# Spectra stage of a fused four-layer kernel: images 0 and 2 placed in the input's tile, the last sample's normalisation moved to ScalarE, a new order of the score products

## The chip, the cores and the metric

The kernel runs on one core of one Trainium2 chip. The metric is the device time of one launch in microseconds (us), the median of several runs. Engines are named as in the profile: PE is TensorE, PEld its weight loads, DVE is VectorE, ACT is ScalarE, POOL is GpSimd, SP is the queue that issues most DMAs.

## The reference, cut to what matters

The input x is (4, 56, 56, 128). Four layers follow, each `x = x + layer(group_norm(x))`: window attention, an edge layer (a message per pair of 56 positions), a spectral attention layer, and a convolution with sums over time and agents. The change lies at the border of the second and third layers and in the first part of the third:

```python
x = x + _L1_conv_ref(_gn(x), ...)          # edge layer
x = x + _L2_conv_ref(_gn(x), ...)          # spectral attention
# inside _L2_conv_ref, _forward:
xa_n = _inorm(xa, norm_g[0], norm_b[0])    # per image (b, t): mean and variance over 56 x 128
k = _fno_layer(xa_n, wK, ..., (H // 2, W // 2))   # rfft2, 16 x 16 modes, weights per head, irfft2
q = _fno_layer(xa_n, wQ, ..., (H // 2, W // 2))
v = _fno_layer(xa_n, wV, ..., (H, W))
scores = einsum('bhtd,bhsd->bhts', qs, ks) / sqrt(d)
attn_w = softmax(scores)                   # 32 heads, 56 x 56 per head and sample
out = einsum('bhts,bhsd->bhtd', attn_w, vs)
# ... then a projection, two more spectral layers with norms, and the residual
```

B is 4 samples; P is 128 channels, on the partitions; HH is 56. One sample is one tile of 128 x 3136 f32, 1568 KB. The kernel never builds k, q and v: it works on the spectra of the images, with the weights of q and k multiplied beforehand.

## The kernel before, in words

**First two layers.** `build` runs `first_layers` once per sample: `fast_layer` (window attention, reads the input tile `xw`) and then `edge_layer`, which works in place on tile `x1`. The result goes to DRAM as `x2d`. Sample b - 1 is normalised for the third layer inside sample b's `fast_layer` by the generator `normed_images`, and written twice, as `xad[b]` and, transposed, as `xat[b]`. All this stands inside a runtime branch (`tc.If`). For the last sample, b = 3, this normalisation is left for the next stage. `xw` lies in the pool `io`, which is released after the branch. In the last edge layer nothing reads `xw` any more.

**Loading.** After the branch, `images(b)` loads `xad[b]` into a tile of pool `x2` in two halves on SP (rows 0 to 28, 29 to 55) and clears one more row on POOL (L2894). The pool has two buffers, so images 0 and 1 are loaded at once, and image 2 goes to the buffer of image 0 when that is free. Image 3 is `x1`.

**Spectra.** `spectra` (L1660 on) has an order written out by hand for PE, ACT and DVE; POOL and SP are ordered by the framework. Three generators are interleaved:

- `norm` is `normed_images` for sample 3: 28 steps of row statistics (`bn_stats`, L1525), then a chain of small operations with four tiny matmuls, then `apply_norm` (L193) on four strips of 128 x 784, the write of `xat[3]` and the factor `st.norm[:, 3, 1]`. `go_on(n)` advances it n steps.
- `first[b]` is `first_transform` of image b, four stages of 56 matmuls (L1616), each with one DVE product (L1618) and one ACT copy (L1620) into tile `s_z`.
- `sample_spectra` of sample b has 13 stages: three with the products for S and iS (L1632, copied out by ACT at L1635), two for R (L1644), eight for xh (L1654, copied out by DVE and ACT in turn, L232 and L230). After its stages 2, 5, 7 and 9 one stage of `first[b + 1]` is issued.

`fill(n)` issues n matmuls on constants (L1682), whose result nobody reads. In the same time POOL prepares weights (`score_weights`, `value_weights`, L1711 to L1769), from DRAM tensors that SP loads (L158), and SP writes their last product as `dd` (L1732).

**Scores.** `attention_weights` walks over a list `seq` of 72 products: for each pair of samples bp (0, 1) and each column c of 16, an item n = 0, whose operand `q_u` DVE makes (L1825), and an item n = 1, whose operand POOL makes (L1823); four more items per pair have theirs from DVE (L1821). Each is 16 matmuls (L1838) into `q_acc`. Operands are made four items ahead. After the last item of pair 0, `collect` (L1857) adds the sums into `sc`, and the generator `softmax` of pair 0 is appended to the list `between`. From the fourth item on each item is followed by one step of `between`: first the steps of `skips` (L1849, L1852), then, in pair 1, softmax steps: max, subtraction (L1864) and exponential (L1865) of two samples, sum and division (L1870 to L1872) of two, and four sets of transposes on PE (L1880) with a copy on ACT (L1882).

After that comes `attend` (L1984 and others) and then `outputs`, which the diff does not touch.

Of the kernel before, what the change touches and what calls it, by code (L numbers as in the profile page):

```python
# [19 lines left out]
P = 128  # L20
# [1492 lines left out]
def normed_images(k, w, st, b, wk, bank, xp, xad, xat):  # L1513

    nc = k.nc

    def tiny(name):
        return wk.tile([P, HH], F32, name="s_" + name, bufs=1)  # L1520

    x = xp[:, :HH, :]
    rows = wk.tile([P, HH, 6], F32, name="s_rows", bufs=1)
    for t in range(HH):
        nc.vector.bn_stats(rows[:, t, :], x[:, t, :])  # L1525
        if t % 2 == 1:
            yield
    mv = wk.tile([P, 2], F32, name="s_mv", bufs=1)
    nc.vector.bn_aggr(mv, rows.rearrange("p a b -> p (a b)"))
    yield  # L1530
    yield
    ps = bank()
    nc.tensor.matmul(ps[:, 0:1], k.g4, mv[:, 0:1], start=True, stop=True)
    yield
    mr = wk.tile([P, 2], F32, name="s_mr", bufs=1)
    t1 = wk.tile([P, 1], F32, name="s_t1", bufs=1)
    nc.vector.tensor_copy(mr[:, 0:1], ps[:, 0:1])
    nc.vector.tensor_sub(t1, mv[:, 0:1], mr[:, 0:1])
    nc.vector.scalar_tensor_tensor(t1, t1, t1, mv[:, 1:2], ALU.mult, ALU.add)
    yield  # L1540
    yield
    ps = bank()
    nc.tensor.matmul(ps[:, 1:2], k.g4, t1, start=True, stop=True)
    yield
    var = wk.tile([P, 1], F32, name="s_var", bufs=1)
    nc.vector.tensor_copy(var, ps[:, 1:2])

    half = [rows[:, :, i] for i in range(6)]
    mean, sq, d = tiny("mean"), tiny("sq"), tiny("d")
    nc.vector.tensor_sub(d, half[1], half[4])  # L1550
    yield
    nc.vector.tensor_mul(d, d, d)
    nc.vector.tensor_add(sq, half[2], half[5])
    yield
    nc.vector.scalar_tensor_tensor(sq, d, HH / 4, sq, ALU.mult, ALU.add)
    nc.vector.tensor_add(mean, half[1], half[4])
    yield "root"
    nc.scalar.activation(t1, var, AF.Sqrt, bias=k.eps)
    yield
    yield  # L1560
    nc.vector.reciprocal(mr[:, 1:2], t1)
    nc.vector.tensor_scalar(mean, mean, 0.5, mr[:, 0:1], ALU.mult, ALU.subtract)
    nc.vector.tensor_scalar_mul(mean, mean, mr[:, 1:2])
    yield
    nc.vector.tensor_scalar(sq, sq, mr[:, 1:2], mr[:, 1:2], ALU.mult, ALU.mult)
    ps = bank()
    nc.tensor.matmul(ps[:, 2:2 + HH], k.ones_c, mean, start=True, stop=True)
    yield
    nc.vector.tensor_copy(st.norm[:, b, 0, :], ps[:, 2:2 + HH])
    nc.vector.tensor_sub(d, mean, st.norm[:, b, 0, :])  # L1570
    yield
    nc.vector.tensor_mul(d, d, d)
    nc.vector.scalar_tensor_tensor(sq, d, float(HH), sq, ALU.mult, ALU.add)
    yield
    ps = bank()
    nc.tensor.matmul(ps[:, 62:62 + HH], k.ones_px, sq, start=True, stop=True)
    yield
    nc.vector.tensor_copy(d, ps[:, 62:62 + HH])
    yield

    def normed():
        for t in range(0, HH, 14):
            apply_norm(k, x[:, t:t + 14, :], x[:, t:t + 14, :], mr)
            if t < 42:
                yield
        nc.sync.dma_start(xat[b].rearrange("t w h -> w t h"), x)
        if b < B - 1:
            nc.sync.dma_start(xad[b], x)

    if b == B - 1:  # L1590
        yield from normed()
    yield "root"
    nc.scalar.activation(d, d, AF.Sqrt, bias=k.eps)
    yield
    yield
    nc.vector.reciprocal(d, d)
    nc.vector.tensor_scalar_mul(st.norm[:, b, 1, :], d, w.ng[:, 0:1])
    yield
    if b < B - 1:
        yield from normed()  # L1600


def first_transform(k, st, b, pools, x, to):

    nc = k.nc
    wk, psum = pools

    z = to[b] = wk.tile([P, 33, 2 * HH], F32, name="s_z")  # L1610
    xf = x.rearrange("p t h -> p (t h)")
    for t0 in range(0, HH, 14):
        ps = psum.tile([P, 512], F32, tag="row", name="s_pr")
        for t in range(14):
            for ri in range(2):
                nc.tensor.matmul(ps[64 * ri:64 * ri + 64, t * 33:(t + 1) * 33],  # L1616
                                 xf[:, (t0 + t) * HH:(t0 + t) * HH + 64], k.fw[:, ri, :], start=True, stop=True)
        nc.vector.tensor_mul(z[:, :, t0:t0 + 14], ps[:, :462].rearrange("p (t f) -> p f t", t=14),  # L1618
                             bc(st.norm[:, b, 1, t0:t0 + 14], 1, 33))
        nc.scalar.copy(z[:, :, HH + t0:HH + t0 + 14], z[:, :, t0:t0 + 14])  # L1620
        yield
# [38 lines left out]
def spectra(k, w, st, xat, images):  # L1660

    nc, tc = k.nc, k.tc
    for t in (st.S, st.iS, st.R):
        nc.gpsimd.memset(t[:, :, :, HH:], 0.0)
    nc.gpsimd.memset(st.x1[:, HH, :], 0.0)
    with ExitStack() as es:
        wk = es.enter_context(tc.tile_pool(name="s_wk", bufs=2))
        psum = es.enter_context(tc.tile_pool(name="s_ps", bufs=3, space=PSUM))  # L1670
        tiny = es.enter_context(tc.tile_pool(name="s_pt", bufs=1, space=PSUM))
        es.enter_context(tc.manual_schedule(engines={mybir.EngineType.PE, mybir.EngineType.Activation,
                                                     mybir.EngineType.DVE}))
        norm = normed_images(k, w, st, B - 1, wk, lambda: tiny.tile([P, 512], F32, name="s_pt"), st.x1, None, xat)
        zs = {}
        first = [first_transform(k, st, b, (wk, psum), st.x1 if b == B - 1 else images(b), zs) for b in range(B)]
        idle = tiny.tile([P, 512], F32, name="s_pt")

        def fill(n):

            for _ in range(n):
                nc.tensor.matmul(idle[:, :3 * P], k.ident, bc(k.ones, 1, 3), start=True, stop=True)  # L1682

        def go_on(n):
            for _ in range(n):
                next(norm, None)
        fill(3)
        go_on(28)
        next(first[0])
        next(first[0])  # L1690
        go_on(1)
        fill(4)
        next(first[0])
        go_on(1)
        next(first[0])
        go_on(2)
        for b in range(B):
            for n, _ in enumerate(sample_spectra(k, st, b, (wk, psum), zs.pop(b))):
                go_on(2)
                if b < B - 1 and n in (2, 5, 7, 9):  # L1700
                    next(first[b + 1])

# [69 lines left out]
def attention_weights(k, I, w, st):  # L1772
# [9 lines left out]
    with ExitStack() as es:  # L1782
# [20 lines left out]
        seq = []  # L1803
        for bp in range(2):
            for c in range(16):
                seq += [(bp, c, 0, None), (bp, c, 1, None)]
                if c in (8, 10, 12, 14):
                    seq.insert(len(seq) - 1, (bp, None, c // 2 % 2, c // 12))

        def make(bp, c, n, b2):  # L1810

# [77 lines left out]
        for n, item in enumerate(seq):  # L1889
# [4 lines left out]
            if item[1:3] == (15, 1):  # L1894
                for i in range(2):
                    collect(item[0], i)
                if item[0] == 0:
# [1 line left out]
                    make(1, 1, 1, None)  # L1899
                    between.append(softmax(0, lambda: psum.tile([P, 4, P], F32, tag="t", name="q_pt", bufs=1),  # L1900
                                           nc.vector.tensor_sub, nc.vector.tensor_mul))
            if n >= 3 and between and next(between[0], 0) == 0:
                between.pop(0)
        for steps in between:
            for _ in steps:
# [892 lines left out]
def build(k, packs, I, out):  # L2798
# [3 lines left out]
    with ExitStack() as es:  # L2802
# [7 lines left out]
        x1p = x1s.enter_context(tc.tile_pool(name="x1p", bufs=1, side="right"))  # L2810
        x1w = x1p.tile([P, HH + 1, HH], F32, name="x1")
        x1 = x1w[:, :HH, :]
        dd = dp.tile([3, 4, 2, 16, NB], F32, name="dd")

        l2p = es.enter_context(tc.tile_pool(name="l2", bufs=1))
# [1 line left out]
        st.x1 = x1w  # L2817
        st.norm = l2p.tile([P, B, 2, HH], F32, name="norm")
        with tc.tile_pool(name="w01", bufs=1) as wp, tc.tile_pool(name="io", bufs=1) as io:
            xw = io.tile([P, TOK], F32, name="xw")  # L2820
            with ExitStack() as pre:
                xs = pre.enter_context(tc.tile_pool(name="i_x", bufs=B - 1))
                x = [xw] + [xs.tile([P, TOK], F32, name="i_x") for _ in range(B - 1)]
# [25 lines left out]
                nc.vector.scalar_tensor_tensor(k.shift, k.mr[:, :, 0], -1.0, k.mr[:, :, 1], ALU.mult, ALU.mult)  # L2849
                small_scores = scores_are_small(k, bounds, wp, wk)  # L2850

            def first_layers(front, x, to, loaded=False):
                if not loaded:
                    nc.sync.dma_start(xw, x)
                xf = io.tile([P, TOK], F32, name="xf")
                st = io.tile([P, 9, 6], F32, name="x1_st")
                front(k, w0, xw, xf, x1, st)
                edge_layer(k, w1, x1, st)
                if to is not None:
                    nc.sync.dma_start(to, x1)  # L2860
# [12 lines left out]
            with small.Else():  # L2873
# [4 lines left out]
                with tc.tile_pool(name="n_x", bufs=2) as xs, tc.tile_pool(name="n_ps", bufs=2, space=PSUM) as psum:  # L2878
                    for b in range(B - 1):
                        xp = xs.tile([P, HH, HH], F32, name="n_x")  # L2880
                        nc.sync.dma_start(xp, x2d[b])
                        for _ in normed_images(k, w2, st, b, io, lambda: psum.tile([P, 512], F32, name="n_ps"), xp,
                                               xad, xat):
                            pass

        x2s = ExitStack()
        x2p = x2s.enter_context(tc.tile_pool(name="x2", bufs=2, side="right"))

        def images(b):
            if b not in loaded:  # L2890
                xp = loaded[b] = x2p.tile([P, HH + 1, HH], F32, name="s_x2")
                for o in (slice(0, 29), slice(29, HH)):
                    nc.sync.dma_start(xp[:, o, :], xad[b, :, o, :])
                nc.gpsimd.memset(xp[:, HH, :], 0.0)  # L2894
            return loaded[b]

        loaded = {}
        for b in range(2):
            images(b)
        nc.sync.dma_start(x2d[B - 1], x1)  # L2900
        l3p = es.enter_context(tc.tile_pool(name="l3", bufs=1))
        load_weights(k, l3p, I, "w3_", w2)
# [50 lines left out]
```

## Time and profile before

| what | value |
|---|---|
| median of the runs | 3492.82 us (3477.65 to 3494.12, 3 runs) |
| the profiled execution's own time | 3507.88 us |
| its span in the trace | 3505.9 us |
| mean granted PE clock | 0.983 |
| last edge layer ends | 2596.7 us |
| spectra stage | 2596.7 to 2694.6 us |
| scores, pair 0 and pair 1 | 2694.6 to 2764 us, 2764 to 2835 us |
| busy over the span | PE 95%, DVE 76%, ACT 61%, POOL 36% |

Times inside the kernel are microseconds from the start of the span of the profiled execution, which was 15 us longer than the median. The spectra and scores together are 239 us, some 7% of the span.

### The profile page before, as it was taken

The numbers are of one execution on the slowest core, as the hardware profiler recorded it, in microseconds if no ns is written. First come the engines' busy times: TensorE is split into PE (matmuls) and PEld (weight loads), VectorE is DVE, ScalarE is ACT, GpSimd is POOL, SyncE is SP. The second block draws the span as 40 slices with busy tenths as digits, with TensorE's granted clock in tenths as the row PEclk, the third lists the DMA queues.
The fourth block names the chain that finished last, engine by engine and source line by source line (L and its number), as shares of the span: only waits on it lengthen the run. The fifth ranks groups of instructions, "written<-read, shape, count | busy, mean of one in ns | idle before, by whom it ended". The sixth has DMA issues, their size and how long they took to land. (4 is left out here: it accounts for less than half of the span.)

```text
span 3505.9 us, 64398 instructions
## 1 busy us (share of the span) xinstructions
PE 3342.7 (95%) x27774; PEld 1447.5 (41%) x27774; DVE 2674.1 (76%) x2563; ACT 2130.6 (61%) x2251; POOL 1278.5 (36%) x784
## 2 busy tenths in 40 slices
PE   6999999999999999999999999999988999999998
PEld 4433333353333435333343543334346433336664
DVE  5588867868888696788859768885975778885766
ACT  4688876668888566788857578886642013215442
POOL 0000007700000590000029200001864778874776
PEclk8999999999999999999999999999998999999999
DMA  2134420023433000534400044332022047743201
GB/s 105 43 88 92 96 53 19 20 59 85 98 88 79 19 1 20 122 89 96 97 24 1 20 96 100 85 85 43 1 104 52 1 95 187 186 105 93 57 18 56
DMA packets 98014, 243.44 MB, mean 69 GB/s; under 512 B 64457, under 2 KB 69833, under 8 KB 92713
## 3 DMA queue, kind: packets, MB, share of 16 engines
q0 software_dynamic: 16128, 102.77, 14.7%
q1 hardware_dynamic: 74872, 123.61, 12.1%
q10 hardware_dynamic: 6720, 12.85, 1.3%
q8 instruction: 221, 3.62, 0.4%
q14 instruction: 73, 0.59, 0.1%
HBM read 79.43 MB, written 31.33 MB: 32 GB/s over the span
## 5 line engine op out<-in xcount | busy, mean ns | idle before, releaser
L830 ACT ACTIVATE f_ring<-f_pm 128x1792 f32<-128x1792 f32 (+1 forms) x764 | 1093.8, 1482 | 226.7 <-PE f_pm L827 179.7
L682 DVE TENSOR_TENSOR f_acc<-f_acc,f_ring 128x1792 f32<-128x1792 f32 x468 | 947.7, 2025 | 191.4 <-ACT f_ring L830 162.0
L827 PE MATMUL f_pm<-f_qT,f_kT 32*128 32x448 f32 x5376 | 723.0, 571 | 9.9 <-ACT f_p L716 4.1
L693 PE MATMUL f_pm<-f_ring,f_va 128*32 128x448 f32 (+1 forms) x6304 | 589.4, 490 | 0.0
L672 POOL DMA_DIRECT2D f_far<-f_ring x112 | 96.6, 862 | 1326.9 <-ACT f_ring L830 1071.8
L1230 POOL TENSOR_TENSOR e_tp<-e_a,e_c 128x1792 f32<-128x1792 f32 (+2 forms) x172 | 480.3, 2844 | 36.9 <-issue 36.9
L1228 DVE TENSOR_TENSOR e_td<-e_a,e_pc 128x1792 f32<-128x1792 f32 (+2 forms) x292 | 478.5, 1707 | 8.8 <-ACT e_c L1216 8.8
L827 PEld LDWEIGHTS f_pm<-f_qT,f_kT 32*128 32x128 f32 x5376 | 260.1, 183 | 412.0 <-ACT f_ring L830 300.8
L693 PEld LDWEIGHTS f_pm<-f_ring,f_va 128*32 128x32 f32 x6304 | 163.8, 109 | 410.1 <-issue 397.8
L1232 ACT ACTIVATE e_tp<-e_tp 128x1792 f32<-128x1792 f32 (+2 forms) x172 | 253.3, 1495 | 97.9 <-POOL e_tp L1230 97.9
L1979 DVE TENSOR_TENSOR u_ud<-u_px,u_d 112x1792 f32<-112x1792 f32 x144 | 263.5, 1864 | 39.8 <-PE u_po L1984 35.5
L1981 POOL TENSOR_TENSOR u_up<-xh,u_d 112x1792 f32<-112x1792 f32 (+1 forms) x72 | 241.0, 3375 | 55.2 <-PE u_po L1984 42.9
L1299 PE MATMUL e_acc<-e_td,t_edge 128*32 128x448 f32 x1952 | 231.6, 542 | 6.6 <-DVE e_td L1228 6.6
L1984 PE MATMUL u_po<-u_ud,AT 112*64 112x448 f32 x1056 | 213.8, 544 | 1.9 <-DVE u_ud L1979 1.9
L1299 PE MATMUL e_acc<-e_tp,t_edge 128*32 128x448 f32 x1184 | 147.9, 543 | 23.6 <-ACT e_tp L1232 23.6
L1984 PEld LDWEIGHTS u_po<-u_ud,AT 112*64 112x64 f32 x1056 | 74.5, 138 | 128.9 <-issue 112.9
L1299 PEld LDWEIGHTS e_acc<-e_td,t_edge 128*32 128x32 f32 x1952 | 61.7, 110 | 142.5 <-issue 93.8
L737 DVE RECIPROCAL f_den<-f_den 128x448 f32<-128x448 f32 x28 | 82.6, 2951 | 45.1 <-ACT f_den L734 45.1
L1823 POOL TENSOR_TENSOR q_u<-iS,q_g 128x1792 f32<-128x1792 f32 x32 | 102.8, 3235 | 28.4 <-PE q_acc L1838 28.4
L1838 PE MATMUL q_acc<-q_u,S 64*64 64x448 f32 x1024 | 106.5, 561 | 4.4 <-DVE q_u L1825 3.3
L813 POOL TENSOR_TENSOR x<-xf,xw 128x343 f32<-128x343 f32 x28 | 25.5, 910 | 226.5 <-DVE xf L802 226.5
L1984 PE MATMUL u_po<-u_up,AT 112*64 112x448 f32 x480 | 104.1, 547 | 2.4 <-POOL u_up L1981 2.4
(522 smaller groups left out, 4550.4 us busy)
## 6 DMA issues: line engine op xcount, KB each, us to landing
f_far<-f_ring POOLq DMA_DIRECT2D x112, 896.0 KB, 6.4
u_d<-dd SPq DMA_DIRECT2D x46, 784.0 KB
f_far<-f_ring SPq DMA_DIRECT2D x28, 896.0 KB
xw<-in_x SPq DMA_DIRECT2D x4, 1568.0 KB
x2d<-x SPq DMA_DIRECT2D x4, 1568.0 KB
xat<-x SPq DMA_DIRECT2D x4, 1568.0 KB
x_xs<-xat ACTq DMA_DIRECT2D x32, 196.0 KB
xm<-x_ev ACTq DMA_DIRECT2D x64, 98.0 KB
```

Source lines behind the costliest of these rows:

```text
L682: nc.vector.tensor_add(e.acc, e.acc, slots(j, c))
L693: nc.tensor.matmul(e.po[heads[h], part], va[o, c, heads[h]], p, start=(c == 0), stop=(c == 23 and part.stop == NB))
L827: nc.tensor.matmul(ss[:, i, :NB], kT[heads[h], c * P:(c + 1) * P], qT[heads[h], blk(j)], start=True, stop=True)
L830: nc.scalar.activation(ring[:, slot:slot + m, :], ss[:, :m, :NB], AF.Exp, scale=scale)
L1228: nc.vector.tensor_tensor(t, am, cm, ALU.max)
L1230: nc.gpsimd.tensor_sub(t, am, cm)
L1232: nc.scalar.activation(tf, tf, AF.Relu)
L1299: nc.tensor.matmul(acc[quarters[r0 + r], :NB], w.S[:, 0, :], t[:, r].rearrange("p l n -> p (l n)"), start=(g == 0), stop=(g == len(turns) ...
L1838: nc.tensor.matmul(acc[bp][i][halves[hb % 2], hb // 2, :NB], x[o], u[o, 8 * hb:8 * hb + 8, :].rearrange("p h t -> p (h t)"), start=first, ...
L1979: nc.vector.tensor_mul(u, bc(px[:, :, :NB], 2, m), dm)
L1981: nc.gpsimd.tensor_mul(u, bc(x, 2, m), dm)
L1984: nc.tensor.matmul(po[64 * b2:64 * b2 + 64, :NB], st.AT[:, 8 * i + h0 + q, 2 * bp + b2, :], u[:, b2, q, :], start=(left == 16), stop=(left ...
```

## The change

The input tile `xw` becomes a tile `xi` with one more row, in a pool of its own that lives until the end of the spectra. In the last sample's call of `first_layers`, between `fast_layer` and `edge_layer`, image 0 is loaded into it (one DMA on SP, one clear on POOL). After the branch only image 1 is loaded into `x2`, now one buffer. Image 2 goes into `xi` after the first transform of image 0, without a second clear.

The order of `spectra` begins with the four stages of `first[0]`, with four fills after the third, and no fills ahead of it. All steps of `norm` now come inside the samples: four per stage in stages 0 to 6 of sample 0, one per stage then, two per stage in stages 9 to 12 of samples 1 to 3. For sample 3 the four strips are normalised by ACT (`Identity` with a scale and a bias, the bias made by one more DVE operation on 128 x 1) in place of DVE.

In the scores, the item n = 1 of pair 0 comes one column later. In pair 1 a step of `between` is taken only at items 42, 46, 50 and so on to 70; one step is still taken at item 35.

```diff
@@ normed_images
+    if b == B - 1:
+        nc.vector.scalar_tensor_tensor(t1, mr[:, 0:1], -1.0, mr[:, 1:2], ALU.mult, ALU.mult)
...
-            apply_norm(k, x[:, t:t + 14, :], x[:, t:t + 14, :], mr)
+            if b == B - 1:
+                nc.scalar.activation(x[:, t:t + 14, :], x[:, t:t + 14, :], AF.Identity, bias=t1, scale=mr[:, 1:2])
+            else:
+                apply_norm(k, x[:, t:t + 14, :], x[:, t:t + 14, :], mr)
@@ spectra
-        fill(3)
-        go_on(28)
-        next(first[0])
-        next(first[0])
-        go_on(1)
-        fill(4)
-        next(first[0])
-        go_on(1)
-        next(first[0])
-        go_on(2)
+        for n in range(4):
+            next(first[0])
+            if n == 2:
+                fill(4)
+        images(2)
         for b in range(B):
             for n, _ in enumerate(sample_spectra(k, st, b, (wk, psum), zs.pop(b))):
-                go_on(2)
+                go_on(4 if b == 0 and n < 7 else 2 if b and n > 8 else 1)
@@ attention_weights
-                seq += [(bp, c, 0, None), (bp, c, 1, None)]
+                seq.append((bp, c, 0, None))
+                if bp or c:
+                    seq.append((bp, c - (not bp), 1, None))
                 if c in (8, 10, 12, 14):
                     seq.insert(len(seq) - 1, (bp, None, c // 2 % 2, c // 12))
+            if not bp:
+                seq.append((bp, c, 1, None))
...
-            if n >= 3 and between and next(between[0], 0) == 0:
+            if n >= 3 and between and (item[0] == 0 or n % 4 == 2 and n > 38) and next(between[0], 0) == 0:
@@ build
+        xwp = x1s.enter_context(tc.tile_pool(name="xw", bufs=1, side="right"))
+        xi = xwp.tile([P, HH + 1, HH], F32, name="xw")
+        xw = xi[:, :HH, :].rearrange("p t h -> p (t h)")
...
-            xw = io.tile([P, TOK], F32, name="xw")
...
+            def first_image():
+                nc.sync.dma_start(xi[:, :HH, :], xad[0])
+                nc.gpsimd.memset(xi[:, HH, :], 0.0)
...
                 front(k, w0, xw, xf, x1, st)
+                if to is None:
+                    first_image()
                 edge_layer(k, w1, x1, st)
...
-        x2p = x2s.enter_context(tc.tile_pool(name="x2", bufs=2, side="right"))
+        x2p = x2s.enter_context(tc.tile_pool(name="x2", bufs=1, side="right"))
...
-                xp = loaded[b] = x2p.tile([P, HH + 1, HH], F32, name="s_x2")
+                xp = loaded[b] = xi if b == 2 else x2p.tile([P, HH + 1, HH], F32, name="s_x2")
...
-                nc.gpsimd.memset(xp[:, HH, :], 0.0)
+                if b < 2:
+                    nc.gpsimd.memset(xp[:, HH, :], 0.0)
...
-        loaded = {}
-        for b in range(2):
-            images(b)
+        loaded = {0: xi}
+        images(1)
```

The other branch, which loads image 0 at its end, does not run with these inputs.

More of the change, by code (lines that the diff above doesn't have):

```diff
@@ L1610, in first_transform @@
     z = to[b] = wk.tile([P, 33, 2 * HH], F32, name="s_z")
-    xf = x.rearrange("p t h -> p (t h)")
+    xf = x().rearrange("p t h -> p (t h)")
     for t0 in range(0, HH, 14):
@@ L1675, in spectra @@
         zs = {}
-        first = [first_transform(k, st, b, (wk, psum), st.x1 if b == B - 1 else images(b), zs) for b in range(B)]
+        first = [first_transform(k, st, b, (wk, psum), lambda b=b: st.x1 if b == B - 1 else images(b), zs)
+                 for b in range(B)]
         idle = tiny.tile([P, 512], F32, name="s_pt")
@@ L2884, in build @@
                             pass
+                first_image()
         x2s = ExitStack()
-        x2p = x2s.enter_context(tc.tile_pool(name="x2", bufs=2, side="right"))
+        x2p = x2s.enter_context(tc.tile_pool(name="x2", bufs=1, side="right"))
         def images(b):
             if b not in loaded:
-                xp = loaded[b] = x2p.tile([P, HH + 1, HH], F32, name="s_x2")
+                xp = loaded[b] = xi if b == 2 else x2p.tile([P, HH + 1, HH], F32, name="s_x2")
                 for o in (slice(0, 29), slice(29, HH)):
                     nc.sync.dma_start(xp[:, o, :], xad[b, :, o, :])
-                nc.gpsimd.memset(xp[:, HH, :], 0.0)
+                if b < 2:
+                    nc.gpsimd.memset(xp[:, HH, :], 0.0)
             return loaded[b]
-        loaded = {}
-        for b in range(2):
-            images(b)
+        loaded = {0: xi}
+        images(1)
         nc.sync.dma_start(x2d[B - 1], x1)
```

## The prediction

> **What bounds the kernel now.** I read the page first (PE is busy 95% of the span, so a gain must come from stretches where PE waits or runs slowly), then the chain of work that ended last, to see where it leaves PE, then the busy times cut by windows. I cut at what the order of the code shows: `first[0]`, then samples 0, 1, 2, 3, then the two halves of the scores and the switch between them. Columns: stretch, its length, busy us (instructions) of PE, PEld, DVE, ACT, POOL, the granted clock, DMA.
>
> ```profile
> 2596.70:2617.00 20.30, 16.02 (x242) 11.77 (x241) 10.31 (x62) 1.74 (x3) 1.10 (x5) 0.83 0.86 293
> 2617.00:2649.30 32.30, 23.15 (x308) 20.17 (x307) 25.27 (x33) 7.29 (x17) 31.03 (x48) 0.80 0.24 96
> 2649.30:2668.20 18.90, 18.53 (x300) 15.40 (x300) 5.38 (x9) 8.70 (x19) 4.72 (x5) 0.89 0.67 125
> 2668.20:2684.80 16.60, 16.60 (x303) 14.69 (x302) 5.08 (x9) 7.70 (x17) 0.00 (x0) 1.00 0.02 4
> 2684.80:2694.60 9.80, 9.50 (x79) 7.86 (x78) 2.67 (x5) 6.04 (x14) 0.15 (x1) 1.00 0.02 5
> ...
> 2764.00:2788.00 24.00, 17.00 (x132) 8.20 (x128) 22.61 (x18) 4.94 (x6) 13.91 (x5) 0.86 0.00 1
> ```
>
> Sample 2 is the yardstick: 303 PE instructions in 16.6 us, no idle time, full clock. Sample 0 has 308 and takes 32.3; the 20.3 us ahead of it hold four stages that take 1.76 us each at full clock. So some 28 us of these 98 are waits and a low clock. The chain in the same window names them:
>
> ```profile
> 2601.51 2.53 issue
> 2604.04 4.74 PE s_pr L1616 x110
> 2608.78 4.71 PE s_pt L1682 x8
> 2613.49 3.41 PE s_pr L1616 x112
> ...
> 2627.10 3.16 PE s_pr L1616 x56
> ...
> 2631.05 13.19 DVE x L193
> ```
>
> L1616 costs 43 ns a matmul in the second line and 30 ns in the fourth: the first half ran at a low clock, as did the fills. Then 13.2 us of DVE in one `apply_norm`. The timeline shows that this is no work:
>
> ```profile
> 2622.46 1.26 DVE L1562 TENSOR_SCALAR s_mean<-s_mean,s_mr 128x56 f32<-128x56 f32 x1
> ...
> 2630.96 13.27 DVE L193 TENSOR_SCALAR x<-x,s_mr 128x784 f32<-128x784 f32 x1
> ...
> 2644.68 1.27 DVE L193 TENSOR_SCALAR x<-x,s_mr 128x784 f32<-128x784 f32 x2
> ```
>
> Two more strips take 1.27 us together; the first stood for 12.6 us while POOL worked without a gap on its weights. DVE is in order: `s_z` and `xh` queue behind the strip, and PE behind them. In the scores, the waits of PE:
>
> ```profile
> PE q_pt L1880 <- DVE y L1872: 5.9, 1, 5.9
> PE q_acc L1838 <- DVE q_u L1825: 3.3, 1, 3.3
> PE q_pg L1849 <- issue: 3.0, 1, 3.0
> ...
> PE q_acc L1838 <- DVE y L1857: 1.1, 1, 1.1
> ```
>
> At the switch of pairs a softmax step follows every product, and PE's transposes wait 5.9 us for DVE's division.
>
> [...]
>
> **The change, part by part** (gain positive, against this execution).
>
> *Image 0 loaded early.* One DMA of 1568 KB goes out on SP when `fast_layer` is done with `xw` (POOL's L815 at 2454.5), 140 us before it is needed; SP issues nothing else in the last edge layer. POOL's clear is 0.23 us in a POOL wait of 9.3 us ahead of L1230. Cost nothing; without that cover 0.23. After the branch SP issues two halves fewer (0.6 us each), so image 1, the write of `x2d` and the weights come sooner.
>
> *First transform.* Before: 20.3 us. After: 1.7 us from the branch to the first matmul, as now (2598.4); the 2.53 us "issue" gap, whose cause the trace does not show (between 0 and 2.5); four stages at 1.76 warm or 2.4 cold (4.74 x 56 / 110), 7.0 to 9.6; four fills, 2.6 warm (the first three took 2.17 with 6 records) to 4.8 cold. Together 11.3 to 18.6; I take 14.3. **Gain 6 (2 to 9).** The three fills and the 6.7 us of `bn_stats` that stood ahead of DVE's first `s_z` leave this place.
>
> *Sample 0.* Before: 32.3. After: the 16.6 of sample 2, plus two tiny matmuls (0.38 each), plus what PE waits for DVE: in stages 0 to 6 DVE has 6.7 us of statistics, two `s_z` (0.64) and a copy (0.61), 8.6 us, against 8.0 us of PE; `bn_aggr` adds 1.66. I take 1.5 us for these. Image 1's first half is needed 3.5 us into the sample, at about 2614; before, image 0's half landed 5 us after issue, so 2602 to 2606 is likely: nothing, at worst 2. No strip on DVE. Sum 19. **Gain 13 (10 to 15).**
>
> *Sample 1.* Before: 18.9, of which 2.3 is the clock. After: 16.6, two tiny matmuls (1.1), a wait for `s_mean` (1.4 before, L1562 to L1567) and one for `s_sq` (1.1 before). These fall at about 2637 to 2645, inside POOL's weights, which start when their loads land, near 2612 to 2617, and take 37 us as now. Then ACT's four strips, two after stage 9 or 10 and two after the next: the trace has no such ACT shape; between 0.58 (128x462, L1620) and 0.95 us (128x896, L1865) I take 0.85, 3.4 together. Behind them on ACT stand `s_z` and `xh` copies, then sample 2's S and iS copies; ACT had 7.7 us of work in 16.6, so it catches up; PE waits some 1.5 us (0 to 3). Sum 21.5. **Loss 2.5 (a loss of 14 to a gain of 1).** The lower end is the strip's own stall, met by L1562.
>
> *Samples 2 and 3.* Matmuls of `first[3]` need `x` and `st.norm` of sample 3: done at stage 0 of sample 2, used at stage 2. **Loss 0.5 (0 to 3).** The write of `xat[3]` is late by nothing: it is read in `attend`.
>
> *Image 2.* Its clear held POOL for 19.2 us before (L2894, until 2617.0); without it POOL's weights start on their data. Its load is issued near 2612 and lands by 2623; first used near 2635. Nothing.
>
> *Scores.* Pair 0's reorder moves nothing off a bound that I can see: PE's 3.0 us "issue" wait lies within `skips`, and POOL at 3.17 us a column keeps pace with PE at 3.1. **Nothing (a loss of 3 to a gain of 4).** Switch: the 24.0 us hold 112 to 116 matmuls of L1838 and 16 transposes. At the steady rate (128 matmuls in 12.31 us, 2788.01 on) that is 11.2, plus 2.6 for the transposes (0.65 each), 13.8; 1.9 us of waiting for `collect` stay. DVE then has, for four products (6.2 us), two operands at 2.02 and one step at 2.2 to 2.4, 6.4: just full, so I add 0.3. **Gain 8 (3 to 10).**
>
> Sum: 6 + 13 - 2.5 - 0.5 + 8 = 24 us, 3507.9 to 3484 for this execution. It was 15 us over the median of the runs, with nothing in it that the change touches as the reason; off the median: 3492.8 - 24 = **3469**. The forecast case by itself is 3459 to 3477.
>
> **Rivals.**
>
> *The lock moves.* L1562, L1563 or L1565 is passed over as the strip was: 12 us in sample 1, PE behind it at the matmul of `s_mean`. For it: they now meet the middle of POOL's work, where two chains of weights alternate. Against: before, L1562 met POOL too and lost 1 us. Gain 24 - 12 = 12: 3481.
>
> *The switch is bound by DVE anyway.* 6.4 us of DVE for 6.2 of PE leaves no room[...]. Gain in scores 2: 3475.
>
> *Slower: image 2 behind `dd`.* SP is in order and waited 31.5 us at L1732 for POOL's last weight; its order is the framework's. If image 2's load is put behind it, it leaves when POOL is done, 2649 to 2660, lands its half 5 us later, and PE stands in sample 1 from stage 2 on. With `dd` at 2660: resume at 2665, then 13.1 + 17.1 + 9.5 = 2704.7, 10.1 later than before, less 8 in the scores: 2 us slower, 3495. It decides from a `dd` later than 2658. Against: SP issued image 2 ahead of `dd` before, at 2616.97.
>
> *The change does not do what it says*: image 0 still waits for the branch's end. Then the first gain goes to 2 and the sum to 20: 3473.
>
> **Numbers.** Forecast 0.55; lock 0.16; switch 0.13; image 2 late 0.08; image 0 unchanged 0.04; something unseen and slower 0.04. From 3450 (the upper ends, 9 + 15 + 1 + 10 = 35 us, and half of the 15 us by which the lowest run lies under the median) to 3487 (the lock with a cold start) holds 8 in 10. About 0.5%, 17.5 us, is what a measurement of this kernel can tell from no change. Faster by more: 0.92 of the forecast, 0.35 of the lock, 0.7 of the switch and of the unchanged image, together 0.69, and 0.72 with some weight for the upper ends. Slower by more: the unseen and a quarter of the late image, 0.06. The rest, 0.22.
>
> **What would show each step.** First transform: `s_pr` from about 2599 without the fills, sample 0 from 2611. Sample 0: 19 us, clock near 1. Lock: an L1562 or L1563 of over 3 us. ACT's strips: four of 0.85 us. Scores: no wait of `q_pt` over 1 us, pair 1 about 61 us after its start. I am wrong if sample 0 stays over 25 us, if PE waits for image 2, or if the last half of the scores is no shorter.

## The result, and the profile after

The change makes the kernel faster: a median of **3473.45 us** (3467.87 to 3478.75) against 3493.33 us for the kernel before (12 runs each), a ratio of 0.994 with an interval of 0.9924 to 0.9956, so 15 to 27 us, and 19.9 by the medians. The profiled execution after took 3474.20 us, its span is 3472.3 us and its mean granted PE clock 0.988.

I cut both traces at the same events: the last product of the edge layer on DVE, the first S product of each sample on PE, the first copy of the scores on ACT, and the two sums of `collect`. All in us:

| stage | before | after | gain | forecast |
|---|---|---|---|---|
| edge layer's end to sample 0 | 20.87 | 24.77 | -3.9 | +6 |
| sample 0 | 31.73 | 16.95 | +14.8 | +13 |
| sample 1 | 19.01 | 17.04 | +2.0 | -2.5 |
| samples 2 and 3 | 26.54 | 27.36 | -0.8 | -0.5 |
| scores, pair 0 | 69.19 | 64.19 | +5.0 | 0 |
| scores, pair 1 | 69.23 | 61.57 | +7.7 | +8 |
| sum | 236.57 | 211.88 | +24.7 | +24 |

The spans differ by more, 33.6 us: the edge layer ended 1.1 us later and the rest of the program, which the diff does not touch, was 10.0 us shorter. That rest took between 660.3 and 672.6 us in the profiles of this document, without a pattern, so I don't count it.

The busy times of after, cut at these events. Columns: stretch, its length, busy us (instructions) of PE, PEld, DVE, ACT, POOL, the granted clock, DMA share, GB/s.

```profile
2597.85:2622.62 24.77, 15.62 (x235) 12.76 (x233) 2.62 (x7) 1.76 (x4) 12.73 (x29) 0.66 0.63 200
2622.62:2639.57 16.95, 16.95 (x305) 15.13 (x305) 13.91 (x68) 7.75 (x17) 16.85 (x23) 1.00 0.17 51
2639.57:2656.61 17.04, 17.04 (x308) 15.18 (x306) 8.96 (x24) 8.75 (x19) 4.55 (x5) 1.00 0.55 139
2656.61:2673.99 17.38, 16.82 (x302) 14.73 (x301) 5.80 (x11) 10.81 (x22) 0.00 (x0) 1.00 0.63 96
...
2748.16:2772.00 23.84, 22.72 (x234) 11.88 (x236) 23.70 (x17) 3.61 (x4) 23.50 (x8) 1.00 0.01 1
```

Samples 0 and 1 now look like sample 2 did before: PE busy from end to end at a clock of 1.00. The first stretch has become worse, 15.62 us of PE work in 24.77 at a clock of 0.66. The chain of waits of after shows what stands in it:

```profile
2600.25 7.09 issue
2607.34 8.64 PE s_pr L1621 x80
2615.99 4.14 PE s_pt L1688 x8
2620.12 1.78 PE s_pr L1621 x56
```

The "issue" gap, 2.53 us before, is now 7.09, and everything behind it up to the end of the fills runs cold, at a granted clock of 0.50 and then 0.67. At the switch of pairs, where PE had waited 5.9 us for DVE's division, the waits of PE over the scores of after no longer have `q_pt`, and `q_pg <- issue` is gone as well:

```profile
PE q_acc L1843 <- DVE q_u L1830: 4.2, 2, 3.3
PE u_po L1989 <- POOL u_up L1986: 2.4, 1, 2.4
PE u_po L1989 <- DVE u_ud L1984: 1.9, 1, 1.9
PE q_acc L1843 <- DVE y L1862: 1.1, 1, 1.1
```

Lines from the timeline of after, of POOL, DVE and ACT, belong together:

```profile
2643.07 1.13 POOL L1732 TENSOR_TENSOR d_f<-d_d 128x448 f32<-128x448 f32 x1
...
2646.08 0.23 DVE L1562 TENSOR_SCALAR s_mean<-s_mean,s_mr 128x56 f32<-128x56 f32 x1
...
2655.86 3.84 ACT L1586 ACTIVATE x<-x,s_t,s_mr 128x784 f32<-128x784 f32 x4
```

POOL's last weight ended at 2644.2 and L1562 ran at 2646.08: the instruction on which I had put the moving stall came after POOL was done. The four strips on ACT take 3.84 us.

### The profile page after: what moved, and what is told of

Its sections match the earlier page's. It is cut to its first block, busy times and chain, and to the rows that moved or that the text cites. A ratio compares the mean times of both kernels' runs of the same rounds, so it can differ in the third digit from the quotient of the medians.

```text
span 3472.3 us, 64384 instructions
## 1 busy us (share of the span) xinstructions
PE 3319.3 (96%) x27768; PEld 1430.6 (41%) x27768; DVE 2658.6 (77%) x2560; ACT 2135.0 (61%) x2255; POOL 1277.5 (37%) x783
## 3 DMA queue, kind: packets, MB, share of 16 engines
q0 software_dynamic: 16128, 102.77, 14.8%
## 5 line engine op out<-in xcount | busy, mean ns | idle before, releaser
L1228 DVE TENSOR_TENSOR e_td<-e_a,e_pc 128x1792 f32<-128x1792 f32 (+2 forms) x292 | 478.3, 1704 | 8.8 <-ACT e_c L1216 8.8
L1828 POOL TENSOR_TENSOR q_u<-iS,q_g 128x1792 f32<-128x1792 f32 x32 | 104.3, 3287 | 13.4 <-PE q_acc L1843 13.3
L2087 ACT COPY x_ev<-x_po 56x896 f32<-56x896 f32 x32 | 28.8, 901 | 126.5 <-DMA x_xs<-xat 44.0
```

What stands on the lines that cost most here:

```text
L1228: nc.vector.tensor_tensor(t, am, cm, ALU.max)
```

## The experiments

Four questions were open. Is the gain of sample 0 that of strips moved off DVE, or of another order? What sets the "issue" gap? Why did pair 0 gain? What is loading image 0 early worth? e1 to e4 ran beside the kernel before at a median of 3485.00 us, e5 to e8 beside it at 3493.28, e9 to e11 at 3486.84. These medians differ by 8 us for one and the same kernel, so across these groups the ratios can be compared and the medians cannot. Stage times come from one profiled execution each. They stand in the order start (the edge layer's end to sample 0), sample 0, 1, 2, 3, pair 0, pair 1. A DVE operation is called passed over when it stands for longer than its work while POOL's operations go on; the "lock" of the prediction and the expectations is this, as the profile of before shows it (13.27 us for one strip).

### e1_strips_on_dve: after, strips on DVE

```diff
-            if b == B - 1:
-                nc.scalar.activation(x[:, t:t + 14, :], ..., AF.Identity, bias=t1, scale=mr[:, 1:2])
-            else:
-                apply_norm(...)
+            apply_norm(...)
```

> The changed kernel, but with sample 3's four strips left on DVE. Theory A (the new order alone ends the 12.6 us stall: the strips now come when POOL's weight work is over, at 2644 in the changed kernel): four strips of about 0.65 us, samples 0 to 3 within 1 us of the changed kernel, total time within 2 us of it. Rival B (moving the strips to ACT ended it): one strip of over 10 us on DVE, about 12 us slower than the changed kernel.

Measured: 3469.93 us, ratio 0.9954 (0.9939 to 0.9969). Stages 23.82, 17.76, 17.04, 16.57, 9.97, 64.21, 61.55. DVE's strips came at 2650 and took 0.64 us each; none was passed over. One small operation in sample 0 was, for 2.00 us (L1538, 128x1), and this sample is 0.8 us longer than in after. So ScalarE is not what saved sample 0. In the new order the strips on ACT cost sample 2 0.8 us (17.38 against 16.57 here) and bring nothing.

### e2_strips_on_act_in_old_order: before, strips on ACT

```diff
@@ normed_images of the kernel before
-            apply_norm(k, x[:, t:t + 14, :], x[:, t:t + 14, :], mr)
+            if b == B - 1:
+                nc.scalar.activation(x[:, t:t + 14, :], ..., AF.Identity, bias=t1, scale=mr[:, 1:2])
```

> The kernel before, with only sample 3's strips moved to ACT. Lock theory: no strip on DVE, so sample 0 falls from 31.7 us to about 19 (the 12.6 us go, the clock stays up) and the kernel is 11 to 15 us faster than before. Rival (DVE or PE was late for another reason, or another DVE operation with SBUF operands inherits the wait): sample 0 stays above 25 us, gain under 6 us.

Measured: 3488.43 us, ratio 1.001 (0.9998 to 1.0023). Stages 21.19, 29.01, 18.34, 16.58, 9.97, 69.2, 69.2. The timeline of DVE in this kernel:

```profile
2634.09 7.93 DVE L1602 TENSOR_SCALAR norm<-s_d,t_images 128x56 f32<-128x56 f32 x1
```

With the strips gone from DVE, the stall took a small operation behind them in the chain, 7.93 us for 128x56 (0.25 us in e8). Sample 0 stayed at 29.01 us, so the expectation of 19 failed. The moving lock of my rivals is real; what e2 doesn't have is the new order.

### e3_scores_order_alone: before, new order of the scores

```diff
@@ attention_weights of the kernel before: the list seq and the condition on between, as in the change
```

> The kernel before, with only the two edits of the scores (n = 1 items one column later in pair 0; softmax steps every fourth item in pair 1). If the 5.0 us that pair 0 lost and the 7.7 us that pair 1 lost in the changed kernel come from these edits: pair 0 about 64 us, pair 1 about 61.5 us, 10 to 13 us faster than before. Rival (pair 0's gain is the 3.0 us wait of q_pg that the profile calls issue, and came and went by chance or with the DMA traffic): pair 0 stays at 69 us in this run and only pair 1 gains, 6 to 8 us faster.

Measured: 3479.71 us, ratio 0.9987 (0.9971 to 1.0003). Stages 22.08, 22.68, 16.57, 16.57, 9.97, 70.4, 61.56. Pair 1 has its whole gain, pair 0 has none. In the medians the 5 us are not clear of the noise. The waits of PE in this kernel's scores, then SP's timeline:

```profile
PE q_pg L1853 <- issue: 4.3, 1, 4.3
```

```profile
2686.77 0.83 SPq L1946 DMA_DIRECT2D u_d<-dd  x2
```

The gap stands in the first `skips` (from 2692.44), which SP's load of `u_d` (1.6 MB) precedes. In after the same load left at another time:

```profile
2647.70 0.91 SPq L1947 DMA_DIRECT2D u_d<-dd  x2
```

The spectra of e3 are those of the kernel before, line for line, and here its strips were hardly passed over (1.29, 2.60 for two, 1.52).

### e4_loads_after_first_transform: after, no load in the first transform

```diff
@@ build
-        nc.sync.dma_start(x2d[B - 1], x1)
-        load_weights(k, l3p, I, "w3_", w2)
...
+                    def later():
+                        nc.sync.dma_start(x2d[B - 1], x1)
+                        load_weights(k, l3p, I, "w3_", w2)
+                        load_weights(k, l3p, I, "w2_", w2, only=CONV_WEIGHTS)
+                        all_score_weights(k, I, w2, sp, wk, st)
+                        value_weights(k, I, w2, wk, dd)
@@ spectra, SP's order by hand too
         images(2)
+        later()
```

> The changed kernel, with SP's loads of weights and its write of x2d held back: SP is in the written order, image 2's load (which waits for the first transform) stands ahead of them. In the changed kernel PE stood still for 7.09 us after its first 10 matmuls behind the branch, a wait that the profile calls issue. Theory C (PE's own instructions arrive late because they share the DMA engines with 2.7 MB that SP has just issued): the gap falls to 3 us or less, the first transform from 24.8 us to about 19, total 4 to 6 us faster than the changed kernel. Rival D (the gap is a fixed cost of running on behind the branch): the gap stays at 6 to 8 us, total within 2 us of the changed kernel. Rival E (the loads held back then make POOL's weights late): PE or POOL wait in the scores for q_g, slower.

Measured: 3488.05 us, ratio 1.0001 (0.9986 to 1.0016). Stages 20.58, 16.94, 31.44, 16.57, 9.97, 67.14, 61.56. The waits of PE up to sample 1's end:

```profile
PE s_pt L1578 <- DVE s_sq L1575: 5.7, 1, 5.7
PE s_pr L1621 <- issue: 3.7, 2, 2.5
```

The gap fell from 7.09 to 2.5 us and the start by 4.2 us. The DMA queues in after from 2598 to 2608, and then all that e4 has from 2595 to 2601 (packets, MB, share of 16 engines):

```profile
q1 hardware_dynamic: 763, 2.91, 90.8%
q14 instruction: 4, 0.03, 1.5%
q8 instruction: 1, 0.02, 0.7%
```

```profile
q14 instruction: 3, 0.02, 1.6%
q8 instruction: 1, 0.02, 1.4%
```

In e4 the instruction queues have the DMA engines alone; in after they share them with 2.91 MB. The price: POOL's weights came late, 2629.10 to 2665.3, and DVE's chain met them in sample 1:

```profile
2645.92 2.74 DVE L1572 TENSOR_TENSOR s_d<-s_mean,norm 128x56 f32<-128x56 f32 x1
...
2649.13 7.32 DVE L1574 TENSOR_TENSOR s_d<-s_d 128x56 f32<-128x56 f32 x1
```

### e5_one_weight_chain_old_order: before, without the values' weights on POOL

```diff
@@ value_weights of the kernel before: its arithmetic on POOL
-    nc.gpsimd.tensor_scalar_add(m, w.V[:, 0], w.pvh[:, 1:2])
...
+    nc.gpsimd.memset(f, 0.0)
```

> The kernel before, but without the arithmetic of value_weights on POOL (dd is written with zeros, so the values' weights, and the output, are not the reference's). POOL is left with one chain of weights, of the scores. Theory A (a DVE operation [...] is passed over as long as POOL's two chains alternate without a gap): no DVE operation of the norm over 3 us in sample 0, sample 0 at 19 to 23 us in place of 31.7 (as in the old order with the scores edit, where it was 22.7 by luck), 8 to 12 us faster than the profiled kernel before, 5 to 10 in the medians. Rival B (sample 0 is slow for PE's own matmul waits and a low clock, whoever runs on POOL): it stays over 27 us, gain under 3.

Measured: 3481.18 us, ratio 0.9974 (0.9959 to 0.9989). Stages 21.89, 25.32, 16.57, 16.57, 9.98, 68.63, 68.51. This kernel leaves out the arithmetic of the values' weights and writes zeros in their place. POOL was done at 2630.73, and no operation of DVE in sample 0 stood for over 1 us, which fits the lock. But e3 and e8, with all of POOL's work, have no long stall either, and sample 0 still took 25.32 us here where both of them took 22.68. So the length of sample 0 in the old order is not the stall alone. Most of the rest is PE's clock: PE was busy for 22.50 of the 25.32 us at a granted clock of 0.80, and for 20.89 of 22.68 us at 0.85 in e3, where after needs 16.95 us at 1.00 for about the same products. What holds the clock down there, no run isolates.

### e6_old_order_of_products: after, old list of products

```diff
-                seq.append((bp, c, 0, None))
-                if bp or c:
-                    seq.append((bp, c - (not bp), 1, None))
+                seq += [(bp, c, 0, None), (bp, c, 1, None)]
...
-            if not bp:
-                seq.append((bp, c, 1, None))
```

> The changed kernel, with the order of pair 0's products undone and the spread of the softmax steps kept. Pair 0 took 69.2 us before and 64.2 after, and 70.4 in the old kernel with both edits of the scores. Theory F (pair 0's 5 us came from the u_d loads: issued at 2698 before, on top of the first skips, and at 2648 after; the order of the products does nothing): pair 0 stays at 63.5 to 65 us, the total within 1.5 us of the changed kernel. Rival G (the order matters once that wait is gone, because POOL's operand is then late at the start): pair 0 at 66 us or more, the total 2 to 4 us slower than the changed kernel.

Measured: 3476.01 us, ratio 0.9955 (0.9939 to 0.9971). Stages 25.02, 16.95, 17.04, 17.38, 9.98, 62.5, 61.56. Pair 0 keeps its gain, and is 1.7 us shorter still, with the old list; `u_d` left SP at 2646.88 here, and there was no gap. The 1.7 us are the first 63 products, 6.27 us here and 7.97 in after; but 63 products also took 7.97 us in e8 with the old list and in e1 with the new. The new list of pair 0 brings nothing that shows.

### e8_before_once_more: the kernel before, unchanged

> The kernel before, unchanged, for a second profile. If the stall of one DVE strip is a matter of chance from run to run, sample 0 differs from 31.7 us by several us (22 to 33), while pair 1 (69.2 us) and the switch of pairs (PE's 5.9 us wait for the division) repeat within 0.3 us. If the stall is fixed by the program, sample 0 repeats within 1 us.

Measured, in one run: 3492.62 us. Stages 22.45, 22.68, 16.57, 16.58, 9.97, 67.07, 69.09. DVE's timeline, where the profiled execution of before had one strip of 13.27 us:

```profile
2628.36 1.20 DVE L193 TENSOR_SCALAR x<-x,s_mr 128x784 f32<-128x784 f32 x1
...
2631.48 2.49 DVE L193 TENSOR_SCALAR x<-x,s_mr 128x784 f32<-128x784 f32 x2
...
2634.44 1.53 DVE L193 TENSOR_SCALAR x<-x,s_mr 128x784 f32<-128x784 f32 x1
```

The same program, and the strips lost some 2.7 us together (5.22 against 4 x 0.64). Its stages sum to 224.4 us, 12.2 less than in the profile that I predicted from. The stall of 13 us is an event of some executions.

### e9_image0_call_behind_branch: after, image 0's load written behind the branch

```diff
                 front(k, w0, xw, xf, x1, st)
-                if to is None:
-                    first_image()
...
+        first_image()
         loaded = {0: xi}
```

> The changed kernel, with the call that loads image 0 moved from the last edge layer to behind the branch. In the changed kernel image 1's load, which is written behind the branch too, left SP at 2457 us, 140 us before the branch ended for PE. If SP runs ahead through the branch and the place of the tile alone decides when a load can leave, image 0's load still leaves at about 2456 to 2458 and the stages are those of the changed kernel within 1 us. If the call's place decides, it leaves at about 2597 and PE waits for it, with the first transform 3 to 8 us longer.

Measured, in one run: 3479.05 us. Stages 24.94, 17.31, 17.04, 17.78, 9.97, 63.9, 61.57. SP's timeline, image 0 first, then the halves of image 1:

```profile
2451.40 0.33 SPq L2860 DMA_DIRECT2D xw<-xad  x1
2452.21 1.09 SPq L2904 DMA_DIRECT2D s_x<-xad  x2
```

Written behind the branch, both left in the middle of the last edge layer, as they do in after (2455.85 and 2457.24), and every stage lies within 0.4 us of after. So where the call stands was of no account here. In the kernel before, SP's first load of an image was released by the last `e_td` of the edge layer on DVE (L1228), after 197.2 us of waiting. The likely reason is that its tile took the place of tiles still in use.

### e11_images_loaded_as_before: after, all images in x2 again

```diff
-        xi = xwp.tile([P, HH + 1, HH], F32, name="xw")
+            xw = io.tile([P, TOK], F32, name="xw")
...
-        loaded = {0: xi}
-        images(1)
+        loaded = {}
+        for b in range(2):
+            images(b)
```

> The changed kernel, with its first part undone: images 0 and 1 in two buffers of x2, loaded behind the branch, image 2 with its clear on POOL. Theory: early loading gave nothing at the start (its gain went into the longer wait for PE's instructions), but it freed POOL 5 us earlier and so ended POOL's weights before DVE's chain. Then the time up to sample 0 is 22 to 26 us, as in the changed kernel (24.8), POOL's weights end 4 us or more after DVE's first norm operations begin, and one DVE operation of over 2 us is seen in most executions: 3 to 10 us slower than the changed kernel, with a wider spread. Rival (early loading is what shortened the start): the time up to sample 0 is 28 us or more, with PE waiting for images.

Measured: 3478.61 us, ratio 0.9988 (0.997 to 1.0005). Stages 22.87, 24.94, 19.52, 17.38, 9.98, 64.19, 61.56. The waits of PE, and the operation of DVE behind the first of them:

```profile
PE s_pt L1543 <- DVE s_t L1539: 7.5, 1, 7.5
PE s_pr L1621 <- DMA s_x<-xad: 4.3, 1, 4.3
...
PE s_pr L1621 <- issue: 2.3, 1, 2.3
```

```profile
2629.60 8.98 DVE L1538 TENSOR_TENSOR s_t<-s_mv,s_mr 128x1 f32<-128x1 f32 x1
```

The start was shorter than in after, by 1.9 us, although PE waited 4.3 us for image 0: the gap behind that wait was 2.3 instead of 7.1. It seems that what PE waits for there comes in while it waits for the image, so that the two waits overlap. The loss came later, in samples 0 and 1, 10.5 us together in this profile. POOL ended its weights 56.0 us after the edge layer here (2591.53 to 2647.54) and 46.3 in after, and DVE's chain ran into them. Two things held POOL's weights. SP sent the first of their loads, `t_w_qk`, at 2607.68, behind the images (in after at 2597.31, ahead of everything else). And POOL stood at the clear of image 2, whose buffer the first transform was still reading:

```profile
2613.78 0.14 POOL L2899 MEMSET s_x<- 128x56 f32 x1 [21.20 <-PE s_pr L1621]
```

The weights began at 2613.89, right behind it. e11 undoes the early load and brings this clear back at once, so it doesn't part the two.

### e7_x2d_after_first_transform and e10_norm_chain_later: going further

e7 is e1, with the write of `x2d` (1568 KB) tied to the end of the first transform by a copy of one column on DVE. e10 is e7 with the chain of `norm` put later and denser.

```diff
@@ e7, spectra, after next(first[0]) of the last stage; the write behind the branch is gone
+        nc.vector.tensor_copy(st.x1[:, 0, 0:1], st.x1[:, 0, 0:1])
+        later()      # nc.sync.dma_start(x2d[B - 1], x1)
@@ e10
-                go_on(4 if b == 0 and n < 7 else 2 if b and n > 8 else 1)
+                go_on((4 if n < 7 else n > 10) if b == 0 else 2 if b == 1 and n > 4 else 1)
```

> The changed kernel with the strips on DVE and the write of x2d[3] (1568 KB) tied to the end of the first transform (by a DVE copy of one column of x onto itself, under 0.2 us); the loads of weights leave when they did. Theory C (PE's instructions share the DMA engines with what SP issued): with 1.2 MB in place of 2.7 MB ahead of them the gap after the first 10 matmuls falls from 6 or 7 us to 2.5 to 4.5, and unlike in the run with all loads held POOL's weights are not late, so no DVE operation of the norm waits over 3 us: 2 to 4 us faster than the changed kernel with the strips on DVE, some 3 to 5 faster than the changed kernel, 18 to 24 us faster than before. Rival (POOL is then still at its weights when the norm's chain, some 4 us earlier, needs DVE): one operation of over 3 us, no gain.

Measured: **3466.22 us**, ratio 0.993 (0.9906 to 0.9954). Stages 22.85, 16.95, 17.04, 16.57, 9.98, 63.21, 61.57. The write left SP at 2616.67, and the gap was 4.9 us where e1 has 6.0. This is the lowest median of all. That it beats the kernel before is shown. That it beats after is likely, but not shown: its interval overlaps that of after, and the two did not run beside each other.

> The kernel with x2d's write after the first transform (strips on DVE), with the steps 29 to 45 of the norm put some 3 us later (none in stages 7 to 10 of sample 0, two per stage from stage 5 of sample 1 on), so that the chain meets POOL only after its weights are done. If waits of DVE behind POOL still cost time there (1.23 us at L1553 in the profile of that kernel), sample 1 stays within 17.5 us and the median is the same or up to 1.5 us lower, with the spread of the runs no wider than 3463.6 to 3471.2. If the denser chain makes PE wait at its tiny matmuls instead, sample 1 becomes 18 to 20 us and the kernel 1 to 3 us slower.

Measured: 3473.09 us, ratio 0.9954 (0.9935 to 0.9972). Stages 22.2, 16.66, 20.74, 16.57, 9.97, 64.2, 61.57. The waits of PE in it:

```profile
PE s_pt L1533 <- DVE s_mv L1529: 1.3, 1, 1.3
PE s_pt L1567 <- DVE s_mean L1563: 1.2, 1, 1.2
```

POOL was done at 2630.81, no operation was passed over, and sample 1 still lost 3.7 us: all four of PE's small products now fall into one sample, in a chain so dense that two of them wait for DVE, 2.5 us together.

## Why the prediction was right, and where it wasn't

The time (3469) was 4 us from the median, and the sum (24) 0.3 us from the profile's stages. Two terms of it hid each other's errors.

**First transform: wrong in sign**, 6 forecast, -3.9 measured. Term by term, after had 1.9 us to the first matmul, 0.5 for the ten recorded ahead of the gap, 7.1 of gap, 8.6 and 1.8 of stages, 4.1 of fills and 0.7 of waiting. The gap failed most: I let it lie "between 0 and 2.5", as if removing what stands near it could only help. In every kernel PE gets 7 to 11 recorded matmuls into the spectra and then stands. What counts is the time from the first of those matmuls to the end of the gap:

| DMA beside it | kernels | first matmul to end of gap | gap |
|---|---|---|---|
| none | e4 | 3.0 us | 2.5 |
| weights | e7, e10 | 5.4 to 5.5 | 4.9 to 5.0 |
| old order: images, `x2d`, 0.2 MB of weights | before, e2, e3, e5, e8 | 5.6 to 6.0 | 2.3 to 2.8 |
| weights and `x2d` | e1, e6, e9, after | 6.5 to 7.9 | 6.0 to 7.4 |

In the old order the three fills and a short wait for the image covered 3 us of it. The change takes them out, and I counted their 2.2 us as a gain, where they had lain beside this wait. (e11, without fills, can be compared from the edge layer's last matmul on: 6.9 us, where the old order takes 6.6 to 7.1, the last row 8.0 to 9.2 and e4 4.2.) That the loads lengthen it is shown by e4, and for `x2d` by e7 against e1 (1.1 us, one profile each). Bytes alone do not set it: the old order issues more, the 3136 KB of two images and 1568 KB of `x2d`, and takes less than the last row. Why stays open. That it is PE's instructions arriving late is an inference and was not shown. What the traces have is the two queues that the profile calls "instruction": in the gaps of before, after, e1 to e5, e7, e8, e10 and e11 q14 moves one or two packets (0.01 to 0.02 MB), and in six of these (before, after, e1, e2, e7, e10) q8 moves one more of 0.02 MB. They do not say whose instructions these are, and no run takes them alone apart.

The other mis-sized term is the cold rate: 2.4 us a stage, read from the profile before, against 8.64 x 56 / 158 = 3.1 us in after. The 2.4 was a mixture: the granted clock over those 4.67 us was 0.69, and the same matmuls in e3, e5 and e8, also with fills ahead, took 6.18 us, 3.1 a stage. And PE stayed cold: cut at these matmuls, after shows

```profile
2607.34:2615.92 8.58, 8.58 (x159) 8.51 (x158) 1.28 (x2) 1.16 (x2) 4.07 (x9) 0.50 0.68 200
2615.92:2620.05 4.13, 4.13 (x9) 2.11 (x8) 0.64 (x1) 0.58 (x1) 3.93 (x8) 0.67 0.26 107
```

8.58 us of matmuls without a pause, at a clock of 0.50. That the clock might be back within the stages, the 1.76 us at the low end of my range, was an estimate; in 8.58 us of these narrow matmuls it did not come back. In after the clock rose only in the wide fills (0.67) and was 1.00 behind them.

**Sample 0: right in size, half right in reason.** 14.8 against 13. "No strip on DVE" was the reason given; e1 has the strips on DVE and takes 17.76. It is the order that does it: the statistics lie beside sample 0, POOL's weights start some 6 us sooner and end 11 us sooner, and the rest of DVE's chain comes when POOL is nearly or wholly done. e2, e4 and e11 each bring the two together in another way, and each has a stall of 7 to 9 us. The stall is not all of it: PE stood idle for 8.7 of the 31.7 us before (5.2 of them for the `xh` that DVE copied right behind the strip), and its 23.0 us of work, at a clock of 0.80, became 16.95 at 1.00. Against e8, which has no long stall, 3.9 of the 5.7 us gained are PE's faster work and 1.8 are waits.

**Sample 1: wrong in sign, small.** A loss of 2.5 forecast (its terms add up to 21.7 us, not 21.5), a gain of 2.0 measured: POOL's weights ended at 2644.2, not about 2650, so `s_mean` waited for nothing, and the strips fell beside the end of the sample. They took 0.96 us each (3.84 / 4), not 0.85, and show in **samples 2 and 3**: -0.8 against -0.5.

**Image 0 and image 2.** "Cost nothing" was right, and the halves of image 2 left at 2613.24 and about 2621.9, well ahead of `dd` (2644.23), so the slower rival did not come. But this part did not pay at the start, where I had put it (e11 starts sooner). It pays in samples 0 and 1, by freeing SP and POOL earlier, the early load and the clear that image 2 no longer needs together. And image 1 came with image 0, which I had not seen: SP ran ahead into the code behind the branch, and the load left at 2457.24 us, 140 us before PE got there.

**Scores, pair 0: missed.** 5.0 us against 0. I had the 3.0 us gap before me and set it at nothing, because it lies within `skips`. In the six kernels that issue the whole load of `u_d` some 5 to 7 us ahead of the first `skips` (before, e2 to e5, e8) it is 2.6 to 4.5 us. In the others at least half of `u_d` had left soon after `dd`, and it is 0. So the gap goes with a load in all thirteen profiles, though no run moves that load alone; and the load's place followed from the spectra's order, not from the list of products (e6). The framework orders SP, and my edit by edit reading asked only what each edit removes, not what SP then issues sooner. Most of the other 2 us are the products behind the gap: 61 took 7.66 us before, 63 took 6.06 in after, while the first 63 took 7.97 in both. No run isolates them.

**Switch: right.** 7.7 against 8, and 61.55 to 61.57 us in every kernel with the new condition. The rival of a bound by DVE is refuted: the row 2748.16:2772.00 has DVE at 23.70 of 23.84 us, full as forecast, and PE still at 22.72.

**Off the median: not sound.** I said of the execution 15 us over the median that nothing the change touches was the reason. e8 shows that 12.2 us of it were in these very stages. Against e8 the stages of after gain 12.5 us, against the profiled execution 24.7; the medians, with 19.9, lie between. The total was right with some luck.

## What to carry to other kernels

Before costing an edit by a stall, ask whether the stall is in every execution: a DVE operation passed over by POOL is priced by its chance (a strip of 13.27 us before and of 1.20 us in e8), and moving it to another engine left the next one in its place (7.93 us, e2), while shifting one of the two chains in time took the meeting away (e1: sample 0 in 17.76 us, no operation passed over for more than 2.00). Where PE stands on "issue", ask what it would have done meanwhile before counting that work as a gain, look at what the DMA engines carry just then, and hold back bulk writes that nobody waits for (the write of `x2d`: 1.1 us, e7 against e1). Ask of each edit also which loads will leave sooner: in e9 the call stood behind the branch and the load left at 2451.40 all the same, so look at the place of its tile.

## What the runs showed of the hardware

- A DVE operation of 128x1 elements stood for 8.98 us in e11 beside a POOL that works without a break (the same operation took 0.16 us in e8). Waits like it lasted over many POOL instructions, 7.3 to 13.3 us, in four profiles (before, e2, e4, e11) and not in the others, the same program among them (before, 13.27 us for one strip; e8, 5.22 us for all four). What decides between them, and what holds DVE, stays open.
- Behind the runtime branch PE came to a stand after some ten matmuls in every profile, for 2.5 us with the DMA engines nearly idle (e4) and for 7.1 us where they moved 2.91 MB beside it (after); in straight code it stood 2.6 to 4.5 us in the six profiles where the whole load of 1.6 MB had just been issued.
- 158 narrow matmuls (128x33) without a pause ran for 8.58 us at a granted clock of 0.50 in after, and for 8.57 us at 0.50 in e7.
- SP issued loads written behind a runtime branch 140 us before PE got there (2457.24 in after, 2452.21 in e9).
